# When the first layer's strips are stored, and in which order VectorE takes residuals, softmax and convolution taps

## The chip, the cores and the metric

The kernel runs on one core of one Trainium2 chip. The metric is the device time of one execution in microseconds, here the median of several runs. The engines of the core are named as the profile names them: PE is TensorE (PEld its weight loads), DVE is VectorE, ACT is ScalarE, POOL is GpSimd, SP is the queue that issues most DMAs.

## What is computed

Eight images of 384 channels and 64 x 64 pixels go through two residual layers, both behind a group normalisation (`_gn`, 32 groups). The first is windowed attention: a layer norm over channels, q, k and v, attention in windows of 8 x 8 for two branches of four heads (the second on an image shifted by four pixels, with a mask), and a projection. The second is a 1 x 1 convolution, a filter in the frequency domain of each 8 x 8 patch, a depthwise 3 x 3 convolution, a gate with Gelu, and another 1 x 1 convolution. Cut to what matters:

```python
x = x + L0(_gn(x))
x = x + L1(_gn(x))

# L0, for each branch, in windows of 64 tokens
attn = softmax(q @ k.T * SCALE + bias + mask)
out = concat(attn @ v, both branches) @ proj_w + proj_b

# L1
t = einsum('bchw,oc->bohw', x, w_in)
t = irfft2(rfft2(patches(t)) * fft_filter)
t = depthwise_conv3x3(t, w_dw)
x1, x2 = t[:, :hid // 2], t[:, hid // 2:]
out = einsum('bchw,oc->bohw', gelu(x1) * x2, w_out)
```

All data is float32.

## The kernel before

An image is worked on in eight strips of 8 rows x 64 columns = 512 pixels. A strip is a tile of 128 partitions x 3 channel groups x 512 pixels, 768 KB. Layer 1 of an image (the second layer, called mixing below) runs beside layer 0 (attention) of the next image: the attention of image b+1 fills the time in which the mixing of image b waits for other engines, and the other way round.

The order is written out by hand. Each piece of work is a small function (`load`, `scores`, `weights`, `project`, `keep`, `conv`, `gate`, `finish`, and so on), and `at(place, piece, ...)` puts it on a plan with a place in units of about half a strip. The plan is sorted by place and then emitted. Matmuls keep the order of the plan (`tc.keep_in_program_order` in the helper at L53). On the other engines a scheduler puts the instructions in an order of its own, from the plan's order and the dependencies. A dependency can be added by hand: one of class Sync makes an instruction wait for another engine, one of class NoSync only orders two instructions of one engine.

Pieces that matter here:

- `load` (L279) brings a strip from memory on the SP queue. There are five kinds: stats and norm from the input, add (the residual of layer 0) from the input, mix and finish from `x1d`, the DRAM buffer with the output of layer 0. All share five buffers of tag x. A load waits for the latest "gate", the ScalarE instruction that moves the first q tile of a branch (`qab`, L367): what comes behind it on TensorE is a stretch of dense 128-row matmuls.
- `weights` (L429 to L434) adds the position bias to the scores (`e<-pS`), takes the maximum `mx` and subtracts it; `exponent` (L439) takes exp on ScalarE; `turn` (L56, `pT`) transposes on TensorE.
- `project` (L516) multiplies with the projection (`pr`) and adds the residual into `x_add`; `keep` (L524) then stores the strip to `x1d` at once and takes its statistics (L220).
- `conv` (L636 on ScalarE for the first tap, L642 on VectorE for the other eight) makes the depthwise convolution `zz` from the padded strip `z`, three channel groups in the order 0, 2, 1. `gate` (L652 to L656) takes Gelu on ScalarE and multiplies on VectorE.
- `finish` multiplies with the output weights (`pw`), adds `x_finish` on VectorE (L672) and stores to the output (L673).
- `mix` (`pt`), `transform` (`pf`) and `back` (`pz`) are the matmuls between.

PSUM holds four buffers of tag gemm with 512 columns each (pq, pvv, pr, pt, pf, pz, pw, ln) and two of tag att with twice that (pS, pT, pA, po). A matmul that takes a buffer waits for the engine that still reads its former content; `pt` comes soon after the three `pw` and takes theirs. In a strip's order on TensorE, pz, pA and pS follow each other as runs of 64 x 64 tiles (many short instructions), then pw, then dense pq, po, pt.

Of the kernel before, what the change touches and what calls it, by code (L numbers as in the profile page):

```python
# [9 lines left out]
ALU = mybir.AluOpType  # L10
AX = mybir.AxisListType

P = 128
# [5 lines left out]
NS = SW // WS  # L19
# [13 lines left out]
def block_kernel(ctx: ExitStack, tc: tile.TileContext, out, x, consts, fsel, wqk, wv, bqk, bv,  # L33
                 wp, bp, lng, lnb, rpb1, rpb2, w_in, w_dw, w_out, filt):
    nc = tc.nc
# [224 lines left out]
    def at(place, piece, *args):  # L260
        plan.append((place, len(plan), piece, args))
# [7 lines left out]
        nc.gpsimd.memset(z[:, :, SW + 1:SW + 2], 0.0)  # L269
    gs0, gs1, st0s, st1s, x1d = ({} for _ in range(5))  # L270

    def load(b, s, what):

        if b == 0 and (what == "stats" or what == "norm" and s < 3):
            xs[b, s, what] = first_x[s]
            return
        t = xs[b, s, what] = strip("x", 5, f"x_{what}_{b}_{s}")
        src = x1d[b][s] if what in ("mix", "finish") else rows_of(x[b], s)
        i = nc.sync.dma_start(out=t, in_=src)  # L279


        if zs.get("gate"):
            tc.add_manual_dep(i.ins, zs["gate"].ins.name, mybir.DependencyInfo(
                mybir.DependencyClass.Sync, mybir.DependencyReason.DATA), reason="load in dense work")


    def input_stats(b, s):
# [132 lines left out]
    def weights(b, s, br):  # L420

        nm = f"{b}_{s}_{br}"
        pS = qks.pop((b, s, br, "S")).rearrange("p o (h w j) -> p o h w j", h=2, j=64)
        e = sb.tile([P, 2 * NS, 64], F32, tag="e", bufs=1, name=f"e_{nm}")
        e5 = e.rearrange("p (h w o) j -> p o h w j", h=2, o=2)
        row = 1 if (br == 1 and s == NS - 1) else 0
        spans = ((0, 0, 4, row),) + (((1, 0, 3, row), (1, 3, 4, 2 + row)) if br == 1 else ((1, 0, 4, row),))
        for odd, a, z, kind in spans:
            nc.vector.tensor_tensor(  # L429
                e5[:, odd, :, a:z, :], pS[:, odd, :, a:z, :],  # L430
                bias_t[br, kind, odd].unsqueeze(2).to_broadcast([P, 2, z - a, 64]), ALU.add)
        mx = small.tile([P, 2 * NS], F32, tag="mx", bufs=2, name=f"mx_{nm}")
        nc.vector.tensor_reduce(mx, e, AX.X, ALU.max)
        nc.vector.tensor_tensor(e, e, mx.unsqueeze(2).to_broadcast([P, 2 * NS, 64]), ALU.subtract)  # L434
        qks[b, s, br, "e"] = e

    def exponent(b, s, br):
# [80 lines left out]
    def keep(b, s):  # L518

        if b not in x1d:  # L520
            x1d[b] = dr.tile([NS, P, KC, ST], F32, tag="x1d", name=f"x1d_{b}")
            st1s[b] = small.tile([P, NS * KC, 6], F32, tag="st1", bufs=2, name=f"st1_{b}")
        t = xs.pop((b, s, "add"))
        nc.sync.dma_start(out=x1d[b][s], in_=t)  # L524
        strip_stats(st1s[b], s, t)


    def second_mean(b):
# [98 lines left out]
    def conv(b, s, m, tap):  # L627

        z = zs[b, s, m]
        n = on_pe[s].get(m, 0) if b == B - 1 else 0  # L630
        if tap < max(n, 1):
            return
        if tap == max(n, 1):
            zz = row512("zz", 5, f"zz_{b}_{s}_{m}")
            if n == 0:
                nc.scalar.activation(zz.rearrange("p (r c) -> p r c", c=SW), z[:, 1:9, 1:SW + 1], AF.Copy,  # L636
                                     scale=dw_sb[:, m, 4:5])
                zs[b, s, "zz", m] = zz
            zs[b, s, "acc", m] = zz
        acc, old = zs[b, s, "acc", m], zs[b, s, "zz", m]  # L640
        dy, dx = TAPS[tap] // 3, TAPS[tap] % 3
        i = nc.vector.scalar_tensor_tensor(acc.rearrange("p (r c) -> p r c", c=SW),  # L642
                                           z[:, dy:dy + 8, dx:dx + SW], dw_sb[:, m, TAPS[tap]:TAPS[tap] + 1],
                                           old.rearrange("p (r c) -> p r c", c=SW), ALU.mult, ALU.add)
        if b < B - 1 and m and tap == 1:
            tc.keep_in_program_order(i)
        zs[b, s, "zz", m] = acc

    def gate(b, s):
# [9 lines left out]
    def finish(b, s):  # L659


        g0, g1 = zs[b, s, "g"]
        t = xs[b, s, "finish"]
        pw = [psum(f"pw_{b}_{s}_{m}") for m in range(KC)]

        for m, half, r in ((0, 0, 0), (1, 1, 1), (0, 1, 0), (1, 0, 1), (2, 0, 0), (2, 1, 1)):
            rows, cols = slice(r * 64, (r + 1) * 64), slice(half * 64, (half + 1) * 64)
            matmul(pw[m][cols], wo_sb[rows, 1, m * P + half * 64:m * P + half * 64 + 64], g1[rows],
                   start=True, stop=False)
        for m in range(KC):  # L670
            matmul(pw[m], wo_sb[:, 0, m * P:(m + 1) * P], g0, start=False, stop=True)
            nc.vector.tensor_tensor(t[:, m, :], pw[m], t[:, m, :], ALU.add)  # L672
        nc.sync.dma_start(out=rows_of(out[b], s), in_=t)  # L673


# [3 lines left out]
    for b in range(B):  # L679
        first = 2 * NS * b  # L680

        for s in range(NS):
            u = first - 14.84 + s if b else -10 + 0.1 * s
            at(u, load, b, s, "stats")
            at(u + (0.5 if b else 0.05), input_stats, b, s)
        if b == 0:
            at(-3.02, pack_qk)
            at(-2.9, qk_weights, 0)
            at(-0.95, v_weights)
            at(-0.94, qk_weights, 1)  # L690
            at(-0.9, position_bias, 0)
            at(-0.5, position_bias, 1)
            at(0.2, out_bias)
            at(0.2, filter_weights)
        at(first - 5.8 if b else -8, input_mean, b)
        at(first - 5.4 if b else -7.9, input_std, b)
        for s in range(NS):
            u = first + 2 * s

            v = u - 4  # L700
            at(v - 0.84, load, b, s, "norm")
            at(v + 0.15, group_normal, b, s)
            at(v + 0.45, ln_square, b, s)
            at(v + 0.99, ln_sums, b, s)
            at(v + 1.35, ln_scale, b, s)

            if s:
                at(v + 1.50, shifted_half, b, s - 1, 1)
            else:
                at(u - 1.15, shifted_half, b, NS - 1, 1)  # L710
            at(u - 1.2 if s < NS - 1 else v + 1.55, shifted_half, b, s, 0)
            for br in range(2):
                w = u + br
                for t in range(3):
                    at(w - 1 + (0.14, 0.34, 0.55)[t], qk_tile, b, s, br, t)
                for g in range(2):
                    at(w - 1 + ((0.78, 0.86), (0.67, 0.88))[br][g], v_tile, b, s, br, g)
                at(w + 0.05, scores, b, s, br)
                at(w + 0.12, weights, b, s, br)
                at(w + 0.30, exponent, b, s, br)  # L720
                at(w + 0.64, turn, b, s, br)
                at(w + 1.00, apply, b, s, br)
                at(w + 1.07, normalise, b, s, br)
                at(w + 1.23, put, b, s, br)

            if 0 < s < NS - 1:
                places = [u + 3 + f for f in (0.27, 0.45, 0.70)]
            else:
                places = [first + 2 * NS + f + (0.0 if s else 0.24) for f in (0.36, 0.44, 0.52)]
            at(int(places[0]) - 0.84, load, b, s, "add")  # L730
            for m in range(KC):
                at(places[m], project, b, s, m)
            at(places[2] + 0.1, keep, b, s)
        first += 2 * NS
        at(first + 1.25, second_mean, b)
        at(first + 1.90, second_std, b)
        if b == B - 1:
            at(first + 2, tap_matrices)
        for s in range(NS):
            u = first + 2 + 2 * s  # L740
            at(u - 0.84, load, b, s, "mix")
            at(u + 0.02, normal_x1, b, s)
            for i in range(4):
                at(u + (0.28, 0.45, 0.60, 0.78)[i], mix, b, s, i)
            for j in range(2):
                at(u + (0.995, 1.02)[j], transform, b, s, j)
            at(u + 1.99, back, b, s)

            for n, m in enumerate((0, 2, 1)):
                for tap in range(1, 6):  # L750
                    at(u + (2.62, 3.15, 3.5)[n] + 0.06 * tap, conv, b, s, m, tap)
                for tap in range(6, 9):
                    at(u + 4.06 + 0.3 * (n * 3 + tap - 6) / 9, conv, b, s, m, tap)
            if b == B - 1:
                at(u + 2.3, conv_taps, b, s)
            at(u + 5.16, load, b, s, "finish")
            at(u + 4.40, gate, b, s)
            at(u + 6.10, finish, b, s)

    for _, _, piece, args in sorted(plan, key=lambda p: p[:2]):  # L760
# [108 lines left out]
```

## Time and profile before

| | |
|---|---|
| median of 3 runs | 3809.83 us (3804.54 to 3810.86) |
| profiled execution | 3803.7 us, its span 3801.9 us |
| granted TensorE clock, mean | 0.994 |
| DMA, mean over the span | 99 GB/s |
| stores x1d<-x_add | 64, 768 KB each, median 3.6 us to landing |
| DVE taps, L642 | 1490, mean 751 ns |
| DVE residual additions, L672 | 192, mean 683 ns (start to start about 600) |
| DVE maximum, L433, and subtraction, L434 | 128 each, mean 1217 and 1232 ns |
| ACT table loads | 1283 ns each |

The span is the time from the first to the last instruction. Busy time is a sum over instructions, and the matmuls' ends are modelled, so a busy TensorE can still run slowly: the granted clock tells that. "issue" as the cause of a gap means that the engine waited for nothing that the profile shows. Queue q1 holds the transfers that the program issues from SP, q8 carries instructions.

### The profile page before, as it was taken

How to read it: one execution, taken by the hardware profiler on the slowest of the kernel's cores; microseconds unless marked ns; L12 is line 12 of the kernel's file. 1: busy time of each engine (PE TensorE's matmuls, PEld its weight loads, DVE VectorE, ACT ScalarE, POOL GpSimd, SP SyncE). 2: the span in 40 equal slices, each digit the busy share in tenths (PEclk: the TensorE clock that was granted, in tenths of full speed). 3: DMA queues.
4: the chain of work that ended last, by engine and by line, in shares of the span. 5: the costliest groups of instructions: out<-in, count | busy, mean ns of one | idle time of the engine just before them, and what ended most of it. 6: DMA issues, size and time to landing. Idle time of an engine off the chain costs nothing.

```text
span 3801.9 us, 90288 instructions
## 1 busy us (share of the span) xinstructions
PE 3681.0 (97%) x39168; PEld 2350.2 (62%) x39168; DVE 2822.1 (74%) x4601; ACT 2458.7 (65%) x3997; POOL 273.0 (7%) x648
## 2 busy tenths in 40 slices
PE   6999999999999999999999999999999999999998
PEld 4666666666666665666666666666666666666554
DVE  5555577768777678777878777778778777677898
ACT  3766577657667576666767666666676667676442
POOL 4000000000000000000000000000000000000000
PEclk9999999999999999999999999999999999999999
DMA  4322222223322223223322323323233222221422
GB/s 120 99 86 83 89 92 102 90 95 115 115 92 93 109 88 121 97 82 112 115 104 103 107 80 107 123 79 107 91 119 107 98 95 73 97 80 71 159 100 75
DMA packets 144496, 377.16 MB, mean 99 GB/s; under 512 B 12308, under 2 KB 12900, under 8 KB 144100
## 3 DMA queue, kind: packets, MB, share of 16 engines
q1 hardware_dynamic: 139952, 370.60, 27.5%
q8 instruction: 308, 5.05, 0.6%
q0 software_dynamic: 2048, 0.15, 0.1%
q10 hardware_dynamic: 2100, 0.63, 0.1%
q14 instruction: 88, 0.72, 0.1%
HBM read 270.54 MB, written 100.79 MB: 98 GB/s over the span
## 4 chain that ended last, share of the span: by engine, by line
PE 82%; DVE 10%; DMA 3%; ACT 2%; issue 2%; SPq 0%; DVEq 0%; ACTq 0%
PE pq L53 22%; PE pt L53 13%; PE pr L53 12%; PE pvv L53 11%; PE pw L53 6%; DVE zz L642 4%; PE pS L53 3%; PE pz L53 3%; PE pT L56 3%; PE pA L53 2%; PE ln L53 2%; PE po L56 2%; PE pf L53 2%; DMA rs<-line 1%; PE pc L53 1%
## 5 line engine op out<-in xcount | busy, mean ns | idle before, releaser
L642 DVE SCALAR_TENSOR_TENSOR zz<-z,dw_sb,zz 128x512 f32<-128x512 f32 x1490 | 1094.8, 751 | 132.5 <-ACT z L601 114.6
L53 PE MATMUL pq<-y,wqk_sb 128*128 128x512 f32 x2160 | 990.6, 596 | 0.4 <-issue 0.4
L53 PEld LDWEIGHTS pq<-y,wqk_sb 128*128 128x128 f32 x2160 | 403.1, 190 | 457.4 <-issue 426.2
L53 PE MATMUL pt<-wi_sb,xn 128*128 128x384 f32 x1536 | 540.7, 490 | 14.5 <-DVE x_finish L672 14.5
L53 PE MATMUL pr<-oT,wp_sb 128*128 128x512 f32 x1152 | 523.5, 593 | 1.1 <-DVE oT L507 1.0
L53 PE MATMUL pvv<-wv_sb,y 128*128 128x192 f32 x2880 | 495.8, 326 | 0.0
L53 PEld LDWEIGHTS pvv<-wv_sb,y 128*128 128x128 f32 x2880 | 471.7, 190 | 36.2 <-issue 21.8
L53 PEld LDWEIGHTS pt<-wi_sb,xn 128*128 128x128 f32 x1536 | 287.9, 191 | 223.8 <-issue 60.0
L367 ACT ACTIVATE qab<-pq,bq_sb,cst 96x512 f32<-96x512 f32 (+1 forms) x256 | 197.2, 770 | 303.0 <-PE pq L53 301.3
L367 ACT ACTIVATE kcd<-pq,vec 32x512 f32<-32x512 f32 x512 | 348.8, 681 | 8.9
L53 PEld LDWEIGHTS pr<-oT,wp_sb 128*128 128x128 f32 x1152 | 210.9, 190 | 225.1 <-issue 210.9
L322 DVE TENSOR_TENSOR lr<-m 128x128 f32<-128x128 f32 x64 | 18.8, 294 | 437.3 <-ACT m L320 437.3
L553 ACT COPY t<-pt 128x384 f32<-128x384 f32 x256 | 122.8, 480 | 194.4 <-PE pt L53 191.8
L401 ACT COPY v<-pvv 128x384 f32<-128x384 f32 x256 | 121.6, 479 | 177.2 <-PE pvv L53 176.9
L367 ACT ACTIVATE qcd<-pq,bq_sb,cst 96x512 f32<-96x512 f32 (+1 forms) x256 | 197.9, 773 | 56.3 <-PE pq L53 49.2
L516 DVE SCALAR_TENSOR_TENSOR x_add<-pr,vec,x_add 128x512 f32<-128x512 f32 x192 | 143.5, 748 | 120.2 <-PE pr L53 118.4
L349 POOL COPY y<-y 128x384 f32<-128x384 f32 x112 | 99.8, 891 | 1741.9 <-PE pvv L53 1243.6
L636 ACT ACTIVATE zz<-z,dw_sb 128x512 f32<-128x512 f32 x183 | 133.2, 732 | 89.0 <-PE pw L53 56.0
L367 ACT ACTIVATE kab<-pq,vec 96x512 f32<-96x512 f32 (+1 forms) x256 | 174.8, 683 | 21.5 <-PE pq L53 19.4
L439 ACT ACTIVATE e<-e 128x1024 f32<-128x1024 f32 x128 | 135.4, 1058 | 74.9 <-DVE e L434 73.8
L53 PE MATMUL pw<-zz,wo_sb 128*128 128x512 f32 x384 | 182.9, 612 | 0.0
L56 PEld LDWEIGHTS po<-cst,o 128*128 128x128 f32 x1024 | 119.7, 141 | 64.2 <-issue 62.8
(139 smaller groups left out, 5286.9 us busy)
## 6 DMA issues: line engine op xcount, KB each, us to landing
x_add<-in_x_dram SPq DMA_DIRECT2D x64, 768.0 KB, 9.6
x1d<-x_add SPq DMA_DIRECT2D x64, 768.0 KB, 3.6
x_mix<-x1d SPq DMA_DIRECT2D x64, 768.0 KB, 4.3
x_finish<-x1d SPq DMA_DIRECT2D x64, 768.0 KB, 4.4
out_dram<-x_finish SPq DMA_DIRECT2D x64, 768.0 KB, 4.5
x_norm<-in_x_dram SPq DMA_DIRECT2D x61, 768.0 KB, 7.4
x_stats<-in_x_dram SPq DMA_DIRECT2D x56, 768.0 KB, 7.5
rs<-line SPq DMA_DIRECT2D x62, 256.0 KB, 3.0
```

The costliest lines, as they stand in the source:

```text
L53: tc.keep_in_program_order(nc.tensor.matmul(*args, **kw))
L56: tc.keep_in_program_order(nc.tensor.transpose(*args, **kw))
L322: nc.vector.tensor_tensor(rc, m[:, 0:P], m[:, 0:P], ALU.mult)
L349: nc.gpsimd.tensor_copy(dst[:, :, :, :, 0:4], src[:, :, :, :, 4:8])
L367: return nc.scalar.activation(dst[to:to + n], pq[of:of + n], AF.Identity, bias=bias[of:of + n], scale=scale)
L401: nc.scalar.copy(v[:, 2 * g:2 * g + 2, :, 0:HD], pvv[:, 0:384].rearrange("p (g h d) -> p g h d", g=2, h=4))
L439: nc.scalar.activation(e, e, AF.Exp)
L516: nc.vector.scalar_tensor_tensor(t[:, m, :], pr, bp_sb[:, m:m + 1], t[:, m, :], ALU.add, ALU.add)
L553: nc.scalar.copy(t1, pt[:, 0:C])
L636: nc.scalar.activation(zz.rearrange("p (r c) -> p r c", c=SW), z[:, 1:9, 1:SW + 1], AF.Copy, scale=dw_sb[:, m, 4:5])
L642: i = nc.vector.scalar_tensor_tensor(acc.rearrange("p (r c) -> p r c", c=SW), z[:, dy:dy + 8, dx:dx + SW], dw_sb[:, m, TAPS[tap]:TAPS[tap] ...
```

## The change

Four edits. The store of a strip leaves `keep` and becomes a piece of its own, `store`, which waits for the latest gate as loads do, and its place is the next unit plus 1.15. The maximum of branch 0 is ordered behind the last residual addition (`x_finish`), if there is a new one. Tap 6 of each channel group is ordered behind the subtraction of the latest softmax, in all images but the last. The places of taps 6 to 8 move from 4.06 to 4.36 on to 4.2 to 4.45, that of the gate from 4.40 to 4.5. `behind` and `in_dense_work` are new helpers; `load` uses the second.

```diff
+    def behind(i, other, kind, reason):
+        tc.add_manual_dep(i.ins, other.ins.name, mybir.DependencyInfo(kind, mybir.DependencyReason.DATA),
+                          reason=reason)
+
+    def in_dense_work(i):
+
+
+        if zs.get("gate"):
+            behind(i, zs["gate"], mybir.DependencyClass.Sync, "transfer in dense work")
+
...
-        i = nc.sync.dma_start(out=t, in_=src)
-
-
-        if zs.get("gate"):
-            tc.add_manual_dep(i.ins, zs["gate"].ins.name, mybir.DependencyInfo(
-                mybir.DependencyClass.Sync, mybir.DependencyReason.DATA), reason="load in dense work")
+        in_dense_work(nc.sync.dma_start(out=t, in_=src))
...
-        nc.vector.tensor_reduce(mx, e, AX.X, ALU.max)
-        nc.vector.tensor_tensor(e, e, mx.unsqueeze(2).to_broadcast([P, 2 * NS, 64]), ALU.subtract)
+        i = nc.vector.tensor_reduce(mx, e, AX.X, ALU.max)
+        if br == 0 and "added" in zs:
+            behind(i, zs.pop("added"), mybir.DependencyClass.NoSync, "residual first")
+        zs["soft"] = nc.vector.tensor_tensor(e, e, mx.unsqueeze(2).to_broadcast([P, 2 * NS, 64]),
+                                             ALU.subtract)
...
-        t = xs.pop((b, s, "add"))
-        nc.sync.dma_start(out=x1d[b][s], in_=t)
-        strip_stats(st1s[b], s, t)
+        strip_stats(st1s[b], s, xs[b, s, "add"])
+
+    def store(b, s):
+        in_dense_work(nc.sync.dma_start(out=x1d[b][s], in_=xs.pop((b, s, "add"))))
...
+
         if b < B - 1 and m and tap == 1:
             tc.keep_in_program_order(i)
+        if b < B - 1 and tap == 6:
+            behind(i, zs["soft"], mybir.DependencyClass.NoSync, "softmax first")
...
-            nc.vector.tensor_tensor(t[:, m, :], pw[m], t[:, m, :], ALU.add)
+            zs["added"] = nc.vector.tensor_tensor(t[:, m, :], pw[m], t[:, m, :], ALU.add)
...
+            at(int(places[2]) + 1.15, store, b, s)
...
-                    at(u + 4.06 + 0.3 * (n * 3 + tap - 6) / 9, conv, b, s, m, tap)
+                    at(u + 4.2 + 0.25 * (n * 3 + tap - 6) / 9, conv, b, s, m, tap)
...
-            at(u + 4.40, gate, b, s)
+            at(u + 4.5, gate, b, s)
```

## The prediction

> **What bounds the kernel now.** I read the page's engine table first, then TensorE's waits, then the timeline around the longest of them. All times are from the one profiled execution (span 3801.9 us; 3803.7 us with what lies around it).
>
> ```profile
> PE 3681.0 (97%) x39168; PEld 2350.2 (62%) x39168; DVE 2822.1 (74%) x4601; ACT 2458.7 (65%) x3997; POOL 273.0 (7%) x648
> ```
>
> TensorE is busy for all but 121 us. Its matmuls are the same before and after, so only that idle time, and time in which it runs at a lower clock, can be won. The waits of TensorE between 60 and 3544 us, which leaves out the start and the last image's end:
>
> ```profile
> PE pS L53 <- issue: 26.4, 29, 1.9
> PE pt L53 <- DVE x_finish L672: 14.5, 11, 2.5
> PE pA L53 <- issue: 7.0, 10, 1.5
> PE pz L53 <- ACT v L401: 5.4, 11, 1.0
> PE pw L53 <- issue: 2.5, 4, 1.1
> ```
>
> Columns: total us, times, longest. By windows the stretch is 3484 us with 3423.8 busy, so 60 us idle: 36 "issue" (no awaited engine), 14.5 on the residual addition, the rest small. One long "issue" gap, on TensorE and on the queue of DMA issues (third fence line), then the DMA view of 1440 to 1450 us in 40 slices of 0.25 us:
>
> ```profile
> 1445.58 0.46 PE L53 MATMUL pS<-kab,qab 64*64 64x64 f32 x12
> 1447.91 0.50 PE L53 MATMUL pS<-kab,qab 64*64 64x64 f32 x18 [1.87 <-issue]
> ...
> 1442.38 0.33 SPq L524 DMA_DIRECT2D x1d<-x_add  x1
> ...
> DMA  0000000000004999999920200000000000003000
> q1 hardware_dynamic: 144, 0.79, 19.8%
> q8 instruction: 2, 0.03, 1.4%
> ```
>
> The store fills the DMA engines from 1443.2 to 1445.6; an instruction packet of q8 follows only then (the 2s), and TensorE, in the middle of its 64x64 matmuls, stops at 1446.04 and resumes 2.3 us after that packet began. I went through all "issue" gaps over 0.15 us: 28 (27.4 us) have an x1d store issued in the 8 us ahead of them, 16 (8.9 us) do not. In 18 of the 28 the q8 packet begins within some 0.2 us of the end of the store's packets, and every gap ends 2.2 to 2.7 us after its q8 packet began (one 3.1). The other wait, VectorE and then TensorE:
>
> ```profile
> 1394.03 1.22 DVE L433 TENSOR_REDUCE mx<-e 128x16 f32<-128x1024 f32 x1
> 1395.28 0.69 DVE L655 TENSOR_TENSOR g<-g,zz 64x512 f32<-64x512 f32 x1
> 1396.00 1.29 DVE L672 TENSOR_TENSOR x_finish<-pw,x_finish 128x512 f32<-128x512 f32 x2
> ...
> 1396.75 3.38 PE L53 MATMUL pt<-wi_sb,xn 128*128 128x384 f32 x6 [2.26 <-DVE x_finish L672]
> ```
>
> pt needs the PSUM buffer of pw, and the addition that frees it stands on VectorE behind the gate's products and the softmax maximum. Such a gap of 1.6 to 2.5 us comes once per image (six), five more are 0.25 to 0.35 us. Last, windows: length, busy of PE, PEld, DVE, ACT, POOL, then granted clock.
>
> ```profile
> 1397.60:1401.00 3.40, 3.40 (x7) 1.68 (x6) 3.37 (x6) 3.38 (x4) 0.00 (x0) 0.50 0.22 79
> 1448.80:1452.20 3.40, 3.40 (x20) 0.78 (x10) 3.40 (x7) 2.56 (x4) 0.00 (x0) 0.50 0.02 5
> 1858.30:1861.70 3.40, 3.40 (x10) 1.89 (x11) 3.40 (x5) 3.38 (x5) 0.00 (x0) 1.00 0.00 0
> ```
>
> After the longest gaps of both kinds TensorE runs 3.4 us at half clock: at 936.8, 1397.6 and 2776.6 after a residual, at 1448.8 and 2367.0 after an "issue" gap. Up to 1.7 us is lost each time beyond the gap. The third row shows that not every 2 us gap brings it.
>
> [...]
>
> **Part 1, the stores.** All 64 stay, 768 KB each; most move on SP's queue from behind the projection to behind the next qab (L367), past one output store. In strip 1442 that is from 1442.4 to about 1458. The waiting store holds x_add and x_stats behind it, which wait for the same qab already, so the added wait is nothing. The three transfers of that stretch (1458.8 to 1467.9, 3.0 us each) become four: x_stats lands near 1470.3. VectorE waits for it there, but idles 7.9 us until 1478 anyway (lr<-m), so this costs nothing; without that cover it would be 2.4 us a strip. TensorE there runs 128-row matmuls, a dozen instructions per 2.7 us, so a fetch held for 2.3 us doesn't starve it. What is won: between fetch start and stall TensorE ran 217 to 244 instructions in the gaps that no transfer touched, but 23 to 180 in most of the held ones. The missing ones at about 120 per us (192 of pz in 1.8 us, 128 of pA in 0.9 us) are the delay that the store caused: for 1446.0 (235-23)/120 = 1.8 of 1.87 us, for 1214.2 (235-166)/120 = 0.6 of 0.86. Summed over the 28 gaps this is about 18 us; some 9 of the 27 remain, and the 9 without a store. Bounds 10 (natural stalls reappear at the held places) to 27.
>
> **Part 2, residuals first.** In the changed program's instruction order the three x_finish stand ahead of mx, and taps 6 to 8 and the products behind the softmax; ahead stand five taps of the next strip's first channel group. At 1394 that removes mx (1.22), two products (1.38) and some taps before the first addition, but the new taps wait for ScalarE's z and zz: I count the first addition from 1394.4 instead of 1396.0. So some 1.6 of each of the six gaps goes and all of the small ones: 6 x 1.6 + 5 x 0.3 = 11, less 1 for what I may have missed: 10 us. Bounds 5 to 14.5. The softmax pays: in strip 1442 two additions (2 x 0.60, start to start) now precede its subtraction, and exp ends near 1459 to 1461 instead of 1458.1; pT needs it at 1469.2, so 8 us of cover. The pair of Gelus leaves ScalarE's queue ahead of exp and goes behind it, which saves table loads (198 in place of 249 rows of loads in the program, 51 x 1.28 = 65 us of ScalarE, off the path). But it lands ahead of qcd: that ends near 1470.6, pvv takes the PSUM buffer at 1472: 1.5 us of cover, the thinnest in the change. If it is gone, each 0.5 us costs 0.5 x 42 strips = 21 us.
>
> **Half clock.** Both kinds of trigger shrink; four of five windows gone are 4 x 1.7 = 7 us; bounds 0 and 8.5.
>
> **Image boundaries.** Strips 0 and 7 store at the boundary: near 1295 and 1310 before, now at 1322.4 in front of x_finish, x_mix, x_norm and x_stats, and x_mix must wait for the landing of strip 0's store (3.6 us median). Four transfers took 1323.3 to 1333.3; six end near 1338. VectorE takes x_norm at 1333.9, so it waits 2 us; but sh and rc no longer stand behind it, and one maximum fewer stands ahead of the additions. I take 0.4 us each, 7 boundaries: 3 us lost (bounds 0 and 42, see the rivals).
>
> **The end.** From the last image's second mean on, VectorE's and SP's order is the same in both programs, so the last 220 us (where VectorE is the bound) don't move. SP's waits and POOL's memsets of z come later by a few us with tens of us of room.
>
> **Sum.** 18 + 10 + 7 - 3 = 32 us: 3803.7 becomes 3771.7. The median of the runs shown is 3809.83, 6.1 above the profiled execution, so I forecast 3809.8 - 32 = 3778.
>
> **Rivals.** Within 0.2% (7.6 us) a measurement can't tell a change.
> (a) Partial: fetches stall in the burst without a store too (16 gaps speak for it) and VectorE stays late through ScalarE. 10 + 5 + 2 - 3 = 14 won: 3796. Against it: the counts of instructions above.
> (b) No gain: the held fetches only move, since four transfers stand where three were, and cluster gaps return. The "issue" gain goes, 5 us of residuals stay, 3 are lost at boundaries: 3808. Against it: no gap over 0.15 us lies in the dense stretch now, though transfers are in flight there.
> (c) Slower: at each boundary SP stands at x_mix with x_norm and x_stats behind it, VectorE waits until 1338.2 in place of 1333.9 (4.3 us), the additions come late by as much, and pt stalls with a half-clock window (1.7): 6 x 7 = 42 lost, 10 more than won: 3820. It decides from 4.6 us a boundary. Against it: sh is free of the wait, x_finish comes before the maximum.
> (d) The change doesn't do what it says: the moved orders are there in the program, so this has no share of its own.
>
> **Chances.** Forecast 0.58 (won 20 to 44), (a) 0.17, (b) 0.12, (c) 0.13. Faster 0.58 + 0.17 = 0.75, same 0.12, slower 0.13. The forecast's own range is 3766 to 3790. The range to hold 8 in 10 goes from 3764 through (a) and half of (b) to 3808.
>
> **What would show it.** TensorE's "issue" waits at pS, pA and pw fall from 36 to about 18 and no x1d store is issued ahead of the rest; pt's wait on x_finish falls from 14.5 to under 5; half-clock windows in the middle fall from five to one or two. I am wrong if a new wait of TensorE on qcd or kcd (L367) appears, if VectorE's idle before y<-x_norm (now 14.4 us) grows by tens of us with TensorE gaps once per image, or if the issue gaps stay without a store near them.

## The result, and the profile after

The changed kernel takes 3786.1 us (median of 4, 3783.99 to 3787.2) against 3807.18 us (3803.25 to 3810.86) for the kernel before on the same chip: ratio 0.9944, 95% interval 0.9927 to 0.9961, 21 us or 0.56% faster. The forecast was 32 us. The profiled execution fell from 3803.7 to 3784.0 us, its span from 3801.9 to 3782.0: 19.9 us to explain.

TensorE's waits of the kernel after, from 60 us to where the last image's end begins (3520 us; it was 3544 before):

```profile
PE pS L53 <- issue: 19.0, 31, 2.3
PE pT L56 <- ACT e L447: 8.4, 7, 1.4
PE pA L53 <- issue: 6.9, 11, 2.7
PE pz L53 <- ACT v L406: 6.0, 13, 0.7
PE pw L53 <- issue: 3.2, 6, 1.1
PE pt L53 <- DVE x_finish L684: 1.4, 4, 0.5
```

Three things are to be read against the list before. The issue waits (pS, pA, pw, and 0.4 at pq before) fell from 36.3 to 29.1 us, so 7.2 were won there and not 18. pt's wait on the residual fell from 14.5 to 1.4: 13.1 won. And a line that was 1.3 us long is now the second: pT waits for exp, 8.4 us, once per image from the second image on. The five half-clock windows in the middle are gone, and a new one has come, at 876.5 us (granted clock 0.51 until 879.9): four fewer, which at 1.7 us each (half of 3.4 us at 0.50) makes 6.8 us. The sum 7.2 + 13.1 + 6.8 - 7.1 = 20.0 us agrees with the span's difference. The 6.8 is a count of windows and not a measurement; TensorE's busy time fell by 6.0 us (3681.0 to 3675.0).

The new half-clock window follows the longest new gap, at an image boundary. TensorE's timeline there (start, duration, instruction, idle time before it), then the DMA view of 868 to 878 us in 40 slices of 0.25 us:

```profile
872.98 1.01 PE L53 MATMUL pA<-v,eT 64*64 64x49 f32 x54
876.65 0.36 PE L53 MATMUL pA<-v,eT 64*64 64x49 f32 x4 [2.66 <-issue]
```

```profile
DMA  9999999899999999999999996000000000000003
q1 hardware_dynamic: 962, 2.38, 62.0%
```

The boundary's transfers fill the DMA engines until 874.4 us; TensorE, in short matmuls, stands from 874.0 to 876.65, some 2.2 us beyond their end. A q8 packet begins only at 874.16 us, 2.49 us before TensorE resumes. I read such a packet as a fetch of TensorE's instructions, because 37 of the 44 issue gaps before end 2.2 to 2.7 us after one began. It is the picture of the store at 1443 us before, now with the six transfers that wait for the same gate. The last of them are loads from the input in packets of 2 KB on average, as the DMA view of 870.2 to 874.2 us shows (packets, MB, share of the 16 engines):

```profile
q1 hardware_dynamic: 758, 1.48, 100.6%
```

At 1790.6 (2.31 us) and 2701.2 (1.56) the transfers end 0.4 us after and 0.6 us before the gap begins; before, these three boundaries had gaps of 0.74, 0.43 and 0.83, 2.0 us together where there are 6.5 now. So of what the stores won elsewhere 6.5 - 2.0 = 4.5 us were given back here.

The pT that waits is the second branch's in the second strip of an image. Why it is late is seen on ScalarE. ScalarE before, then after:

```profile
1374.16 1.28 ACT L439 ACT_TABLE_LOAD   x1
1375.70 1.06 ACT L439 ACTIVATE e<-e 128x1024 f32<-128x1024 f32 x1 [0.26 <-DVE e L434]
```

```profile
1373.88 1.28 ACT L447 ACT_TABLE_LOAD   x1 [1.84 <-DVE e L441]
1375.18 1.06 ACT L447 ACTIVATE e<-e 128x1024 f32<-128x1024 f32 x1
```

Before, the table load ran while ScalarE waited for VectorE's subtraction, and exp ended at 1376.76, only 0.3 us ahead of pT (1377.09). After, the load itself waits for the subtraction, so its 1.28 us come behind it, and pT, next in order at 1375.16, waits 1.13 us. The groups by line show that this happens in more places: over the whole execution ScalarE's idle time ahead of these loads (last column, with what ended most of it) rises from 6.7 to 99.0 us. Before, then after:

```profile
L439 ACT ACT_TABLE_LOAD x117 | 150.1, 1283 | 6.7 <-DVE e L434 5.4
```

```profile
L447 ACT ACT_TABLE_LOAD x72 | 92.4, 1283 | 99.0 <-DVE e L441 98.6
```

Elsewhere pT comes late enough to hide it. The reason lies in what exp has to wait for. In the instruction records of the trace before, 107 of the 128 exp wait for VectorE, and no wait for VectorE stands ahead of their table load. In the trace after only 62 do; the other 66 wait for an earlier instruction of ScalarE itself, and for VectorE in a separate wait ahead of that. In 51 of the 66 this wait stands right ahead of the table load (before, in 5). By the program the second thing to wait for is ScalarE's own previous exp, since both use the one buffer e; the experiment on the table load tries that.

### The profile page after: what moved, and what is told of

Same layout as the page of the kernel before. It is cut to its first block, busy times and chain, and to the rows that moved or that the text cites. A ratio compares the mean times of both kernels' runs of the same rounds, so it can differ in the third digit from the quotient of the medians.

```text
span 3782.0 us, 90249 instructions
## 1 busy us (share of the span) xinstructions
PE 3675.0 (97%) x39168; PEld 2347.3 (62%) x39168; DVE 2819.9 (75%) x4601; ACT 2379.1 (63%) x3946; POOL 272.9 (7%) x648
## 3 DMA queue, kind: packets, MB, share of 16 engines
q1 hardware_dynamic: 139952, 370.60, 27.8%
## 4 chain that ended last, share of the span: by engine, by line
PE 87%; DVE 5%; ACT 4%; DMA 2%; issue 2%; SPq 0%; ACTq 0%; DVEq 0%
PE pq L53 24%; PE pt L53 13%; PE pr L53 13%; PE pvv L53 12%; PE pw L53 7%; PE pS L53 3%; PE pA L53 3%; PE pz L53 3%; PE pT L56 3%; PE po L56 3%; PE ln L53 2%; DVE zz L651 2%; PE pf L53 2%; PE pc L53 1%; DMA rs<-line 1%
## 5 line engine op out<-in xcount | busy, mean ns | idle before, releaser
L372 ACT ACTIVATE qab<-pq,bq_sb,cst 96x512 f32<-96x512 f32 (+1 forms) x256 | 197.8, 773 | 400.0 <-PE pq L53 398.3
L372 ACT ACTIVATE kcd<-pq,vec 32x512 f32<-32x512 f32 x512 | 348.4, 680 | 9.0
L372 ACT ACTIVATE qcd<-pq,bq_sb,cst 96x512 f32<-96x512 f32 (+1 forms) x256 | 197.0, 769 | 43.9 <-PE pq L53 40.6
L372 ACT ACTIVATE kab<-pq,vec 96x512 f32<-96x512 f32 (+1 forms) x256 | 174.1, 680 | 8.8 <-PE pq L53 7.1
L56 PEld LDWEIGHTS pT<-cst,e 128*128 128x128 f32 x1024 | 119.3, 141 | 66.9 <-issue 40.1
L441 DVE TENSOR_TENSOR e<-e,mx 128x1024 f32<-128x1024 f32 x128 | 158.0, 1234 | 2.5
```

The costliest lines, as they stand in the source:

```text
L56: tc.keep_in_program_order(nc.tensor.transpose(*args, **kw))
L372: return nc.scalar.activation(dst[to:to + n], pq[of:of + n], AF.Identity, bias=bias[of:of + n], scale=scale)
L441: zs["soft"] = nc.vector.tensor_tensor(e, e, mx.unsqueeze(2).to_broadcast([P, 2 * NS, 64]), ALU.subtract)
```

## Experiments

Each ratio is to the kernel before on the same chip, with its 95% interval. Issue waits are the sum over TensorE's list, in one profiled execution each, from 60 us to where the last image's end begins; a few us between two of them say little.

**The two halves of the change.** First the VectorE orders without the stores, then the stores without the orders.

```diff
-        strip_stats(st1s[b], s, xs[b, s, "add"])
+        t = xs.pop((b, s, "add"))
+        nc.sync.dma_start(out=x1d[b][s], in_=t)
+        strip_stats(st1s[b], s, t)
...
-            at(int(places[2]) + 1.15, store, b, s)
```

> The changed kernel with the stores back in keep, ungated: VectorE's orders alone. Theory A (the parts add up as the two traces differ): pt's wait on x_finish 14.5 falls to about 1.5 (13 won), the three half-clock windows that followed it go (5 won), pT's new wait on exp of 8 us once per image is here too (8 lost), TensorE's issue waits stay at 36: about 10 us won, ratio to before 0.997. Theory B (the new pT wait comes from the stores, which delay the transfers of rs): pT's wait is under 2 us here, and about 18 us are won, ratio 0.995.

Measured: ratio 0.9982 (0.9975 to 0.9989), some 7 us. pt's wait on x_finish 1.6 us, pT's on exp 8.5 us, issue waits 40.2 us, one half-clock window.

```diff
-        if br == 0 and "added" in zs:
-            behind(i, zs.pop("added"), mybir.DependencyClass.NoSync, "residual first")
...
-        if b < B - 1 and tap == 6:
-            behind(i, zs["soft"], mybir.DependencyClass.NoSync, "softmax first")
...
-                    at(u + 4.2 + 0.25 * (n * 3 + tap - 6) / 9, conv, b, s, m, tap)
+                    at(u + 4.06 + 0.3 * (n * 3 + tap - 6) / 9, conv, b, s, m, tap)
...
-            at(u + 4.5, gate, b, s)
+            at(u + 4.40, gate, b, s)
```

> The changed kernel without its VectorE orders (residual, taps, places): gated stores alone. Theory A: issue waits 36 fall to about 29 (7 won), the two half-clock windows behind issue gaps go (3 won), pt's wait on x_finish stays at 14 to 15, pT's wait on exp stays under 2: 6 to 10 us won, ratio 0.998. Theory B: pT's wait of 8 us appears here, so that next to nothing is left, ratio 1.000. The step of the prediction (18 won by the stores) would be issue waits of about 18 and a ratio of 0.994.

Measured: ratio 0.9971 (0.9961 to 0.9981), some 11 us. Issue waits 26.8 us, x_finish 13.7, pT 1.3. Four half-clock windows are left in the middle with the stores alone, three of them behind a wait on x_finish. So theory A held in both for who carries what: the stores carry the issue waits, the VectorE orders carry the residual and pT's new wait, and the two gains (0.18% and 0.29%) nearly add up to the whole (0.56%). It missed on one point: the orders alone won 7 us and not 10, and the issue waits did not stay at 36 us with them but were 40.2. The boundary gap at 874 us is there with the stores alone (2.30 us) and absent with the orders alone.

**The table load.** The last copy of v, which stands ahead of the load on ScalarE, takes up the wait for the previous exp.

```diff
-        nc.scalar.activation(e, e, AF.Exp)
+        zs["exp"] = nc.scalar.activation(e, e, AF.Exp)
...
-        nc.scalar.copy(v[:, 2 * g:2 * g + 2, :, 0:HD],
+        i = nc.scalar.copy(v[:, 2 * g:2 * g + 2, :, 0:HD],
...
+        if g == 1 and "exp" in zs:
+            behind(i, zs.pop("exp"), mybir.DependencyClass.Sync, "exponent seen")
```

> The changed kernel, where ScalarE's copy of the second half of v also waits for ScalarE's own previous exp, so that the next exp has only VectorE's subtraction to wait for and the table load ahead of it nothing. Theory A (pT is late because the table load, 1.28 us, waits for the subtraction): table loads ahead of exp no longer idle before on e (98.6 us in the changed kernel), pT's wait of 8.4 us falls under 1.5, 7 to 8 us won against the changed kernel, ratio to before 0.9925. Rival (pT is late because y<-rs, 1.76 us, stands ahead of the subtraction on VectorE): pT's wait stays above 6, ratio as the changed kernel's 0.9944.

Measured: ratio 0.9919 (0.9906 to 0.9931). pT's wait is gone from the list, and the load waits for nothing:

```profile
L449 ACT ACT_TABLE_LOAD x72 | 92.4, 1283 | 1.3
L449 ACT ACTIVATE e<-e 128x1024 f32<-128x1024 f32 x128 | 135.3, 1057 | 68.7 <-DVE e L443 67.5
```

The waiting has moved from the load to exp itself. All 128 exp now wait for VectorE alone, and none has a wait ahead of its load. y<-rs (1.76 us) still stands ahead of the subtraction, so the rival falls. The step in the ratio, from 0.9944 to 0.9919, is some 10 us, but the two intervals overlap a little (0.9927 to 0.9931). Below, the same repair on top of another one takes 0.9936 to 0.9906, with intervals that don't overlap.

**Which of VectorE's two orders does it?** The changed kernel without the order of the taps and their places, then without the order of the residual:

```diff
-        if b < B - 1 and tap == 6:
-            behind(i, zs["soft"], mybir.DependencyClass.NoSync, "softmax first")
...
-                    at(u + 4.2 + 0.25 * (n * 3 + tap - 6) / 9, conv, b, s, m, tap)
+                    at(u + 4.06 + 0.3 * (n * 3 + tap - 6) / 9, conv, b, s, m, tap)
...
-            at(u + 4.5, gate, b, s)
+            at(u + 4.40, gate, b, s)
```

> The changed kernel without the order of the taps (softmax first) and without the moved places of taps and gate: gated stores and the maximum behind the residual. Theory A: the order of the residual alone carries VectorE's gain, pt's wait on x_finish is under 2 us, and about 0.9945. Rival: without the taps behind the softmax the additions are still late (pt's wait over 6), or the softmax comes so late that pT waits more than the 8.4 us of the changed kernel; ratio 0.996 or above.

```profile
PE pt L53 <- DVE x_finish L682: 9.3, 15, 1.1
PE pT L56 <- ACT e L447: 8.1, 7, 1.6
```

```diff
-        if br == 0 and "added" in zs:
-            behind(i, zs.pop("added"), mybir.DependencyClass.NoSync, "residual first")
```

> The changed kernel without the order 'residual first': gated stores, taps 6 to 8 behind the softmax, their places and the gate's. Theory A (the taps carry VectorE's gain, the residual's order carries pT's new wait): pt's wait on x_finish is under 4 us although one maximum and one subtraction stand between the additions, pT's wait on exp is under 2 us since the table loads ahead of exp wait for nothing in all but 13 cases, ratio to before 0.992 to 0.993. Rival (the two orders only work together): pt's wait stays at 8 us or more with half-clock windows, ratio 0.995 or above.

```profile
PE pt L53 <- DVE x_finish L682: 2.4, 6, 0.5
PE pT L56 <- ACT e L445: 1.1, 1, 1.1
```

Ratios 0.9966 (0.9953 to 0.9978) and 0.9937 (0.9923 to 0.9950). The residual's order alone takes pt's wait only from 13.7 to 9.3 and brings the late table loads (98.2 us of idle time ahead of them); against the stores alone (0.9971) it wins nothing that can be told. The taps and products behind the softmax take pt's wait to 2.4 although a maximum still stands ahead of the additions and a subtraction between them, and the loads wait little (10.6 us). Without the residual's order the kernel is as fast as with it (0.9937 against 0.9944, the intervals overlap): of the 7 us that pT's wait gives back the times show some 3, inside the intervals. The second execution ran more of its first 65 us at half clock than the others, so its span doesn't settle the rest.

**The boundary.** Strips 0 and 7 stored at once, then both repairs together.

```diff
-        in_dense_work(nc.sync.dma_start(out=x1d[b][s], in_=xs.pop((b, s, "add"))))
+        i = nc.sync.dma_start(out=x1d[b][s], in_=xs.pop((b, s, "add")))
+        if 0 < s < NS - 1:
+            in_dense_work(i)
...
-            at(int(places[2]) + 1.15, store, b, s)
+            at(int(places[2]) + 1.15 if 0 < s < NS - 1 else places[2] + 0.1, store, b, s)
```

> The changed kernel, where strips 0 and 7 of an image are stored at once behind the projection, as in the kernel before, and only strips 1 to 6 wait for dense work. Theory A (the group of six transfers at an image boundary holds TensorE's instruction fetch): the issue gaps at three boundaries (2.66, 2.31, 1.56) fall under 1 us each, the half-clock window near 876 goes, 4 to 6 us won against the changed kernel, ratio to before 0.993. Rival (these gaps are the natural length of a fetch that falls into short matmuls): they stay or turn up at another place, ratio 0.9944 within 0.0007; or the early stores hold other fetches and it is slower.

> The changed kernel with both repairs: the next exp's wait on ScalarE itself taken up earlier (table load free), and strips 0 and 7 stored at once. If the two losses are separate, they add: against the changed kernel 8 us for pT and 4 to 6 for the boundary gaps, ratio to before 0.9905 (about 3768 where before is 3804). Rival: the boundary gaps and pT's lateness overlap on TensorE (a late TensorE hides a late exp), ratio as with the free table load alone, 0.992.

Measured: 0.9936 (0.9924 to 0.9949) and 0.9906 (0.9891 to 0.9922). With the first edit issue waits fall from 29.1 to 26.0 us, the longest from 2.7 to 1.1, and no half-clock window is left in the middle; with both they are 24.7. The trace bears theory A out, and the times go its way, but each step that the boundary makes in them (3 us, and 5 on top of the free table load) lies inside its interval.

**Is it the size of a store's packets?** The VectorE orders with ungated stores, each made as three transfers:

```diff
-        nc.sync.dma_start(out=x1d[b][s], in_=t)
+        for m in range(KC):
+            nc.sync.dma_start(out=x1d[b][s][:, m, :], in_=t[:, m, :])
```

> VectorE's orders alone with the ungated store of a strip made as three transfers, one for each channel group, in pieces of 2 KB instead of 6. Theory A [...]: [...] issue waits fall from 40 us towards the 29 us of gated stores, ratio to before 0.9965 against 0.9982 with one transfer. Rival (what counts is that 768 KB are in flight, in whatever pieces): issue waits stay at 37 to 43, ratio 0.998 or, with more queueing, higher.

TensorE's longest wait with one transfer, then with three:

```profile
PE pS L53 <- issue: 27.3, 28, 2.0
```

```profile
PE pS L53 <- issue: 16.6, 29, 1.2
```

Ratio 0.9940 (0.9927 to 0.9952) against 0.9982, and all issue waits together fall from 40.2 to 23.5 us, 16.7 less. That brings the ratio as far as gating did (0.9944, with the boundary's loss), and it is more than theory A had said (0.9965). The three transfers make 432 packets of a store in place of 144 (158384 on q1 in all, 139952 in the kernel before), 1.8 KB on average in place of 5.3. But the edit changes more than the size. The queue of DMA issues in the same strip, with one transfer and with three (the view merges the three issues into one line, from the first to the end of the last):

```profile
1439.61 0.33 SPq L532 DMA_DIRECT2D x1d<-x_add  x1
```

```profile
1424.76 10.27 SPq L533 DMA_DIRECT2D x1d<-x_add  x3
```

Each part waits for its own channel group only. In most strips the parts leave some 10, 7 and 0.5 us ahead of pz, the single store 0.2 to 2.5 us ahead. So two thirds of the bytes are gone before the short instructions begin; here the last third keeps the DMA engines busy until 1436.35 us, and the fetch (the q8 packet) begins only at 1437.09. With one transfer it began at 1442.66, as the store's last packet ended. The gain is shown, its cause isn't: smaller packets, or fewer bytes at the wrong time. To part the two, the three would have to leave together just ahead of pz; that was not tried. The boundary at 874 us speaks against the packets: there a fetch began only at 874.16, when TensorE already stood, though the engines had moved packets of 2 KB for 4 us.

On top of both repairs, where the stores of strips 1 to 6 meet dense work, it should do little:

> The version with both repairs, with every store of a strip to x1d made as three transfers of one channel group each (pieces of 2 KB). Theory A: the gated stores meet no short instructions, so that the piece size no longer matters for strips 1 to 6; only the ungated stores of strips 0 and 7 and the boundary could gain, at most 2 us: ratio 0.990 to 0.991, issue waits 22 to 26. Rival [...]: issue waits fall to 18 or less and the ratio to 0.989.

Measured: 3764.7 us, ratio 0.9898 (0.9883 to 0.9913), issue waits 25.4: theory A. This is the fastest version here, though not told apart from both repairs alone (0.9906). In strips 1 to 6 the three parts leave within about 1 us of each other here, but far from short instructions, so this run doesn't part the two causes either.

**What are the 25 us that stay?** With both repairs, 31 of the 40 issue gaps have no packet but those of instructions from 4 us before the gap to its end; they make 18.8 of the 24.7 us. So most of what stays needs no transfer. Three ways to cut the run of pz, pA and pS (384 short instructions) in two were tried. First, in the changed kernel, pz ahead of pT:

```diff
-            at(u + 1.99, back, b, s)
+            at(u + 1.58, back, b, s)
```

> The changed kernel with the place of back (pz) moved from 1.99 to 1.58 of its strip, so that pz's 192 short instructions run ahead of pT and pvv instead of directly ahead of pA and pS (192 more). Theory A (the issue gaps left are fetches that cannot keep up[...]): [...] the issue waits fall from 29 us to under 8, with or without transfers near; if nothing else gets late, ratio to before 0.988. Rival (the gaps belong to pS and pA themselves or to transfers near them): issue waits stay over 20. Either way pvv or pT may wait for PSUM or ScalarE, since z is moved out earlier; that would be a new wait at pvv, pr or pT and could eat the gain.

```profile
PE pz L53 <- ACT kcd L372: 23.7, 13, 3.1
PE pr L53 <- ACT kcd L372: 11.6, 22, 0.9
PE pS L53 <- issue: 2.9, 8, 0.5
PE pA L53 <- issue: 0.8, 2, 0.5
```

Then, with both repairs, the last pr between pz and pA (the strip's statistics later, and x1d set up in store):

```diff
-                places = [u + 3 + f for f in (0.27, 0.45, 0.70)]
+                places = [u + 3 + f for f in (0.27, 0.45, 0.995)]
...
-            at(places[2] + 0.1, keep, b, s)
+            at(places[2] + (0.305 if 0 < s < NS - 1 else 0.1), keep, b, s)
```

> The version with both repairs, and the last of a strip's three projections (pr, strips 1 to 6) moved from between pT and pvv to between pz and pA: 192 short instructions, then 1.8 us of 128-row matmuls, then 192 short ones; the strip's statistics on VectorE follow later. Theory A [...]: the issue waits, 24.7 us with both repairs, fall to under 10 (what is left comes from strips 0 and 7, whose projections stand elsewhere), and since no PSUM buffer is asked for earlier than before, no new wait of over 5 us appears: ratio to before 0.986 to 0.988. Rival: the addition x_add, now on VectorE right ahead of the normalisation and the softmax, makes them late, and po, pq or pT wait; ratio 0.990 or above.

```profile
PE pz L53 <- ACT v L406: 32.5, 34, 1.8
PE pr L53 <- ACT v L406: 17.9, 11, 2.4
PE pS L53 <- issue: 5.6, 10, 1.2
PE pA L53 <- issue: 3.3, 5, 1.1
```

Last, with both repairs and stores in three, back at u + 1.50, ahead of the third pq:

> The version with both repairs and stores in three pieces, with pz moved from 1.99 to 1.50 of its strip, ahead of the third pq and pT: the run of 384 short instructions is cut in two, and pz takes PSUM buffers that ScalarE emptied earlier than at 1.58 (there it waited 36 us for kcd). Theory A: issue waits 25 us fall under 6, the waits of pz and pr on kcd stay under 10 us together and no image brings a half-clock window: about 12 us or more won, ratio to before 0.986 to 0.987. Rival: ScalarE, with z's moves now ahead of qcd and the eT copy, makes pr, pvv or pA wait by more than the 20 us won: ratio 0.990 or above.

```profile
PE pq L53 <- DVE x_add L526: 35.3, 39, 2.2
PE pq L53 <- ACT kcd L372: 28.1, 13, 4.2
PE pz L53 <- DVE gs_b L231: 10.6, 6, 1.9
PE pS L53 <- issue: 1.3, 4, 0.5
PE pA L53 <- issue: 0.8, 2, 0.5
```

Ratios 0.9977 (0.9966 to 0.9988), 1.0025 (1.0017 to 1.0034) and 1.0056 (1.0044 to 1.0068): all three miss as improvements. But the issue waits fell to 3.7, 9.1 and 2.1 us, as theory A had it: what stays in the changed kernel comes with the run of short instructions itself. A rival would be that the new waits give the fetch time to catch up. In the first of the three runs it falls: 19 of its 54 strips with pz have no such wait over 0.15 us, and none of the 19 has an issue gap over 0.15 us; in the changed kernel 27 of the 40 strips without such a wait have one. The stall can't be bought off in these ways. Each moved piece (pz, or the last pr) now takes PSUM buffers that ScalarE or VectorE has not yet emptied, which makes waits of 35, 50 (pz waited 6 of them before) and 63 us (and 11 for gs_b in the last); in the first and the last five and six half-clock windows came back in the middle.

## Why the prediction was right in sign and too large

- **The stores, 18 us (bounds 10 to 27): the term that was mis-sized.** Between the two traces the issue waits fell by 7.2 us, below the bounds. That is not the stores' own share, because the VectorE orders alone raise these waits from 36.3 to 40.2 us. (Why was not tried; one execution each may not tell.) The stores alone took off 9.5 us (36.3 to 26.8), on top of the orders 11.1 (40.2 to 29.1), and 14.2 with strips 0 and 7 stored at once (26.0), since at the boundary six transfers together now hold the fetch. The step that failed is the stall that is there without a transfer. I let TensorE run 235 instructions between the start of a fetch and the stall if nothing holds the fetch, from gaps "that no transfer touched" with 217 to 244. Of nine such gaps in the trace before, three had 80, 141 and 162. In the 31 untouched gaps with both repairs it ran 145 to 242, on average 198. With 198 in place of 235 the same sum over the 28 gaps gives some 12 us (an estimate from these traces), and the part that stays grows from 9 to some 15 of the 27 us. That natural stalls come back at the held places was my lower bound and rival (a); it is what happened. "No x1d store is issued ahead of the rest" came true; "about 18" did not. One more reading was too neat: 37 of the 44 gaps end 2.2 to 2.7 us after their fetch began, but five took 2.9 to 3.25, and two (at 139 and 432 us) have no fetch near them. The sum doesn't rest on it.
- **Residuals first, 10 us (5 to 14.5): measured 13.1, but the mechanism was half wrong.** I put the maximum (1.22 us), two products (1.38) and some taps into one sum. The additions ahead of the maximum win only some 4 of the 13.7 us by themselves. The taps and products behind the softmax take the wait to 2.4 without them, and the order that I named the part after isn't needed.
- **"The softmax pays ... 8 us of cover": the other step that failed.** The cover was read in one ordinary strip, for branch 0. For the second branch in the second strip of an image, where no mixing stands between pq and pT, it was 0.3 us, and the cost was no longer queue on VectorE but a table load of 1.28 us that stopped being hidden. It costs 7.1 us. The count of table loads was right (51 fewer, ScalarE's busy time 2458.7 to 2379.1 us) and worth nothing, as said; what one of them waits for mattered.
- **Half clock, 7 us: 6.8 by the count of windows.** I had one of the five stay; all five went and a new one came at a boundary, so the match is in part luck. The five windows before follow gaps of 1.87 to 2.27 us, the new one a gap of 2.66 us; a gap of 2.31 us in the changed kernel was followed by none (granted clock 1.00 from 1792.9 to 1796.3 us).
- **Boundaries, 3 us lost through VectorE's wait for x_norm.** That wait grew from 14.4 to 21.1 us over all boundaries, and TensorE doesn't show it; rival (c) is far from its 4.6 us each. The boundary's loss (4.5 us, part of the stores' term above) came through the instruction fetch, which I had cleared because "a fetch held for 2.3 us doesn't starve" TensorE in dense rows: true for strips 1 to 6 (the list after has no issue wait at pq, po or pt), but the boundary's longer group of transfers reaches into the next run of short matmuls.
- **Gelus ahead of qcd, 1.5 us of cover:** no wait of TensorE on qcd or kcd (L372) appeared.

The sum 18 + 10 + 7 - 3 = 32 became 7.2 + 13.1 + 6.8 - 7.1 = 20.0. The measured 21 us lie between the forecast and rival (a), at the lower end of what the forecast's own case had allowed. That they lie inside it at all owes something to luck: the residuals won 3 us more than forecast, by a mechanism that was half wrong.

## What to carry to other kernels

Read the cover of a moved step in the strip where it is thinnest, not in a typical one: here it was 0.3 us at one place of each image, and 8 us in the strip that was read. When an order changes, look at what each hidden table load waits for: one more dependency can put an engine's wait on the load instead of on the instruction behind it (here ScalarE's idle time ahead of the loads rose from 6.7 to 99.0 us). Before moving a large transfer out of the way of the instruction fetch, see whether it can leave in parts, each as soon as it is ready (here the issue waits fell from 40.2 to 23.5 us, and gating took them to 29.1). And read how much of the stall is there without any transfer from all gaps that no transfer touches, not from the mildest ones.

## What the runs showed of the hardware

- A 768 KB store just ahead of a run of short instructions delays the q8 packet, read here as TensorE's instruction fetch: the packet begins as the store's last one ends (1445.58 us before, 1442.66 with the VectorE orders alone; within some 0.2 us in 18 of the 28 gaps before that have a store ahead), and with the stores out of the way the issue waits fall from 40.2 to 29.1 us. Amid packets of 2 KB on average (1.48 MB in 758) one began late too, at 874.16 us, when TensorE already stood. What makes it wait was not shown.
- In the runs of 384 short instructions TensorE also stops with no transfer near (18.8 us in 31 gaps with both repairs); with the run cut in two of 192 it does so much less (2.1 to 9.1 us of issue waits against 24.7 to 29.1).
- Long gaps don't always bring a half-clock window: with the free table load two gaps of 2.48 and 2.70 us were followed by none, while 2.66 us brought one in the changed kernel. What decides stays open.
- A table load (1.28 us) can come to stand behind the wait for VectorE of the exp that follows it: right behind it in 51 of 128 exp in the changed kernel and in 5 before, with 99.0 and 6.7 us of ScalarE's idle time ahead of the loads, and in none, with 1.3 us, once an earlier instruction took up the second wait.
